# Head of a fused Mamba and mixture-of-experts kernel: early B and C loads, softplus ahead of the third gate, four C products by VectorE

## The chip, the cores and the metric

The kernel runs on one core of one Trainium2 chip. The metric is device time in microseconds (us) of one execution, the median over runs. Engine names are those of the profile: PE is TensorE (PEld its weight loads), DVE is VectorE, ACT is ScalarE, POOL is GpSimd, SP is SyncE, whose queue (SPq) issues most of the DMAs.

## The reference

Two branches read the same layer-normed input of 4096 tokens with 256 features, and their product is added to the input. All is float32.

```
xn = layernorm(x)                          # x: (2, 2048, 256)
u  = silu(conv4(in_proj_x(rmsnorm(xn))))   # 512 channels
dt = softplus(dt_proj(x_proj_dt(u)));  B, C = x_proj_BC(u)   # 16 states
h_t = exp(dt_t * A) * h_{t-1} + (dt_t * u_t) * B_t           # per channel and state
y_t = sum_s h_t[s] * C_t[s] + D * u_t
s  = xn + out_proj(y * silu(z));  s = s + mlp(rmsnorm(s))
g  = silu(top2_of_8_experts(xn))
out = x + s * g
```

## The kernel before

Tokens are cut into 8 blocks of 512 (c = 0 to 7, four to a sequence), channels into 4 groups of 128 (d), and the 16 states into 8 pairs (g). One scan step n is one (c, d, g): 256 steps. A step makes the input b = du*B on DVE (L1498), two hardware scans on DVE (L1502), one per state, needs two exponentials da from ACT (L1387), which run two steps ahead (LEAD), then the product with C (L1430, in `times_c`, on POOL, the last step on DVE), for most steps from n = 8 the sum of the pair on POOL (L1432), and PE adds the states into PSUM with the identity (L1400). `save` (L1424) keeps the last column of h for the next block.

All work of one engine stands in one order, the order in which the Python program emits it. Three things set that order. Before the scan loop a list of calls is written out by hand (from L1249): `norm`, `logits`, `layer_norm`, `gate` and `scatter_group` for the tokens, `go(k)`, which takes k pieces of the generator `front(0)`, and `tick()`, which lets deferred work (`later`) fall due. In the loop, after each of the 512 half steps, `draw` takes 1.93 us worth of PE work from the first of five lists that has any: `pre` (the last gate and the tables of the experts), `zs` (`gate_z`), `projs` (`out_proj`), `chain` (`front`), `side` (the 39 expert tiles and 16 tiles of the MLP; `side` waits until `pre` is empty). Deferred work falls due some half steps after it was put.

The parts that the change touches or that the prediction follows:

- `norm(b)` scales a block of x on ACT (L277) and transposes it on PE (L288) into PSUM: even blocks into the tile `b` that later holds the scan's input, odd blocks into `du` and `y`. `logits(b)` copies the transposes to SBUF on ACT (L295), stores them (L297) and computes the expert logits on PE (L300). `layer_norm(b)` writes the layer-normed block (blocks 2 to 7 on ACT, L315) and stores it (L321).
- `gate(g)` (L405 to L444) chooses two experts for 1024 tokens on DVE, with two matmuls for the counts (L421, L424); its first operation that reads the counts is a copy, L428. `scatter_group(g)` sends those tokens to their experts' rows by 16 indirect DMAs issued by POOL (L462).
- `front(c)`: four input projections on PE (L621), convolution taps (ACT L631 to L638, DVE L646), SiLU on ACT (L660), `project_x` (PE L666, ACT copy L671, store of B and C to DRAM `bcd`, L673), then per channel group the softplus: `exp_v` (PE L685, ACT L693 to L699, a subtraction L700) and `log_v` (ACT logarithm L707, then L712 and L713 make dt). For c = 0, d = 0 and 1, L700, L712 and L713 run on DVE, otherwise on POOL.
- `load_bc` (L762) loads two rows of `bcd`, broadcast to 128 partitions (512 KB), into the tiles B0 to B7 and C0 to C7. Blocks 0 to 5 of x lie in B0 to B5 at the start, and the transposed blocks 2 to 7 in C2 to C7; B6, B7, C0 and C1 are free.
- `gate_z` (PE L772, ACT L781, L787, L794, DVE L783) makes the gate silu(z).
- `routed` (list `pre`): the last `layer_norm`s and gate 3, the last scatters, `tiles_of_experts` and `rows_of_results` (DVE, L502 to L598), `fill_up` (zeros behind each expert's rows, L604, SPq), and the first expert's loads. An expert reads its rows (L1035), transposes them (PE L934, ACT copy L937) and runs two matmul layers (PE L946 and L958, ACT L1053).

Of the kernel before, what the change touches and what calls it, by code (L numbers as in the profile page):

```python
# [9 lines left out]
F32 = mybir.dt.float32  # L10
# [8 lines left out]
P = 128  # L19
T = 512  # L20
# [32 lines left out]
def kernel(  # L53
# [135 lines left out]
    def with_exp():  # L189
        if table[0] == WITH_SILU:  # L190
            act_table(WITH_TANH)
# [81 lines left out]
    def norm(b):  # L273
        xr = work.tile([P, J, DM], F32, tag="h", name=f"xr{b}")
        for j in range(J):
            i = b * J + j
            nc.scalar.activation(  # L277
                xr[:, j, :], x_of(b, j), AF.Identity,
                scale=both_norms[:, i : i + 1], bias=off[:, i : i + 1],
            )  # L280
        if b % 2:
            pt = [ps_1.tile([P, T], F32, tag=tag, name=f"pt{b}_{tag}") for tag in ("du", "y")]
        else:
            both = ps_b.tile([P, KM, T], F32, tag="b", name=f"pt{b}")
            pt = [both[:, k, :] for k in range(KM)]
        for k in range(KM):
            for j in range(J):
                nc.tensor.transpose(pt[k][:, ts(j, P)], xr[:, j, ts(k, P)], ident)  # L288
        pts[b] = pt

    def logits(b):
        pool, tag = (bcp, f"C{b}") if b > 1 else (rows, "xrT")
        xrT[b] = pool.tile([P, KM, T], F32, tag=tag, name=f"xrT{b}")
        for k in range(KM):
            nc.scalar.copy(xrT[b][:, k, :], pts[b][k])  # L295
        if b > 1:
            nc.sync.dma_start(xrd[b], xrT[b])  # L297
        for j in range(J):
            for k in range(KM):
                nc.tensor.matmul(  # L300
                    lgp[:, b * J + j, :], xrT[b][:, k, ts(j, P)], gw_sb[:, k, :],
                    start=(k == 0), stop=(k == KM - 1),
                )

    def layer_norm(b):

        for j in range(J):
            i = b * J + j
            if b < GB:
                nc.gpsimd.tensor_scalar(  # L310
                    x_of(b, j), x_of(b, j), rstd[:, i : i + 1], moff[:, i : i + 1],
                    ALU.mult, ALU.add,
                )
            else:
                nc.scalar.activation(  # L315
                    x_of(b, j), x_of(b, j), AF.Identity,
                    scale=rstd[:, i : i + 1], bias=moff[:, i : i + 1],
                )
        per = J // len(xts[b])
        for k, xn in enumerate(xts[b]):  # L320
            nc.sync.dma_start(xnd[b][:, ts(k, per), :], xn)  # L321
# [150 lines left out]
    def scatter_group(g):  # L472
        for i in range(g * GI, (g + 1) * GI):
            for k in range(TOPK):
                scatter(i, k)
# [138 lines left out]
    def front(c):  # L614
# [48 lines left out]
        def project_x():  # L663
            px, n = bank("h", [DR + 2 * DS, T], f"pxd{c}")
            for d in range(ND):
                nc.tensor.matmul(  # L666
                    px, xp_sb[:, d, :], xcs[c, d], start=(d == 0), stop=(d == ND - 1)
                )
            xd = rows.tile([DR + 2 * DS, T], F32, tag="xd", name=f"xd{c}", bufs=1)
            bcd[c] = dram.tile([2 * DS, T], F32, tag="bcd", name=f"bcd{c}")  # L670
            later.put(lambda: nc.scalar.copy(xd, px), n)  # L671
            later.put(
                lambda: nc.sync.dma_start(bcd[c], xd[DR : DR + 2 * DS, :]), ("bcd", c), after=3  # L673
            )
            return xd, n

# [79 lines left out]
    def load_bc(c, g, which_ones="BC"):  # L756
        later.free("bcd", c)
        for which in which_ones:
            i = "BC".index(which)
            t = bcp.tile([P, 2, T], F32, tag=f"{which}{g}", name=f"{which}{c}_{g}")  # L760
            r = i * DS + 2 * g
            nc.sync.dma_start(  # L762
                t, bcd[c][r : r + 2, :].unsqueeze(0).to_broadcast([P, 2, T])
            )
            bct[c, which, g] = t
# [475 lines left out]
            later.put(total, after=1 if self.c == NBLK - 1 else 2)  # L1241


    def tick():
        later.now += 1
        later.run()
# [20 lines left out]
    def go(pieces):  # L1267

        for _ in range(pieces):
            next(first)  # L1270
# [25 lines left out]
    logits(4)  # L1296
    tick()
    go(3)
    logits(5)
    layer_norm(4)  # L1300
    layer_norm(5)
    tick()
    norm(6)
    gate(2)
    scatter_group(2)
    tick()
    norm(7)
    go(4)
    logits(6)
    tick()  # L1310
    logits(7)
    assert 0 in bcd and (0, 1) in dt_made
    for which, gs in (
        ("B", (0, 1, 6, 7)), ("C", range(DS // 2)), ("B", (2, 3, 4, 5)),
    ):
        for g in gs:
            load_bc(0, g, which)

# [20 lines left out]
        for _ in ffns[0].rows():  # L1339
            pass  # L1340


    hs, ys, y_n, hts, das, dus = {}, {}, {}, {}, {}, {}

    def all_ffn(upto):

# [24 lines left out]
    zs, projs, chain = [], [], []  # L1371
    side = []
    pre = []

    NS = NBLK * ND * (DS // 2)
    at = [(c, d, g) for c in range(NBLK) for d in range(ND) for g in range(DS // 2)]

    def exps(n, q):
        if n >= NS:
            return  # L1380
        c, d, g = at[n]
        begun[0] = n
        assert (c, d) in dt_made
        if q == 0:
            das[n] = work.tile([P, 2, T], F32, tag="da", name=f"da{c}_{d}_{g}", bufs=3)
        with_exp()
        nc.scalar.activation(  # L1387
            das[n][:, q, :], dts[c, d], AF.Exp, scale=a_neg[:, d, 2 * g + q : 2 * g + q + 1]
        )

    def accumulate(n):
        c, d, g = at[n]
# [28 lines left out]
    def save(n):  # L1421
        c, d, g = at[n]
        if c % CPB != CPB - 1:
            nc.gpsimd.tensor_copy(hs[c][:, d, 2 * g : 2 * g + 2], hts[n][:, :, T - 1])  # L1424

    def times_c(n):
        c, d, g = at[n]

        engine = nc.vector if n == NS - 1 else nc.gpsimd
        engine.tensor_tensor(hts[n], hts[n], bct[c, "C", g], ALU.mult)  # L1430
        if paired(n):
            nc.gpsimd.tensor_tensor(hts[n][:, 0, :], hts[n][:, 0, :], hts[n][:, 1, :], ALU.add)  # L1432
# [24 lines left out]
                share -= got  # L1457
        return min(share, 0.0)

    LEAD = 2  # L1460
    LAG = 3
    BACK = 3
    HALF = 1.93

    pre.append(routed())
    side.append(all_ffn(None))
    for n in range(LEAD):
        for q in range(2):
            exps(n, q)
    owed = 0.0  # L1470
    for n in range(NS):
        c, d, g = at[n]
        if n == 3:
            chain.append(first)
        if d == 0 and g == 0 and c % CPB != CPB - 1:
            hs[c] = small.tile([P, ND, DS], F32, tag="hs", name=f"hs{c}")
        if d == 0 and g == (1 if c else 4):
            zs.extend(gate_z(c, k) for k in range(ND))
        if c + 1 < NBLK:
            if d == 0 and g == 1 and c:  # L1480
                xrT[c + 1] = rows.tile([P, KM, T], F32, tag="xrT", name=f"xrTr{c + 1}")
                nc.sync.dma_start(xrT[c + 1], xrd[c + 1])
            if d == 0 and g == 4:
                chain.append(front(c + 1))
        if c > 0 and d == 0 and g == 0:
            projs.append(out_proj(c - 1))
        if n == NS - 4:
            projs.append(out_proj(NBLK - 1))
        for q in range(2):
            later.now += 1  # L1490
            if q == 0:
                if g == 0:
                    assert (c, d) in dt_made
                    dus[c, d] = ps_1.tile([P, T], F32, tag="du", name=f"du{c}_{d}")
                    nc.vector.tensor_tensor(dus[c, d], dts[c, d], xcs[c, d], ALU.mult)
                hts[n] = work.tile([P, 2, T], F32, tag="h", name=f"h{c}_{d}_{g}")
                inp = ps_b.tile([P, 2, T], F32, tag="b", name=f"b{c}_{d}_{g}")
                nc.vector.tensor_tensor(  # L1498
                    inp, dus[c, d].unsqueeze(1).to_broadcast([P, 2, T]),
                    bct[c, "B", g], ALU.mult,  # L1500
                )
            nc.vector.tensor_tensor_scan(  # L1502
                hts[n][:, q, :], das[n][:, q, :], inp[:, q, :],
                0.0 if c % CPB == 0 else hs[c - 1][:, d, 2 * g + q : 2 * g + q + 1],
                ALU.mult, ALU.add,
            )
            if q == 0 and n > 0:
                save(n - 1)
                times_c(n - 1)
            exps(n + LEAD, q)  # L1510
            later.run()
            if q == 0 and n >= LAG:
                sums(n - LAG)
            if q == 0:

                past = n - BACK
                if past >= 0 and at[past][1] == ND - 1 and at[past][0] + 1 < NBLK:
                    load_bc(at[past][0] + 1, at[past][2])
            owed = draw(HALF + owed)
# [66 lines left out]
```

## Time and profile before

| what | value |
|---|---|
| median of 3 runs | 1506.11 us (1504.72 to 1514.64) |
| the profiled execution | 1505.4 us; its span 1503.7 us |
| PE busy | 1347.4 us (90% of the span), mean granted clock 0.944 |
| DVE busy | 1217.2 us (81%) |
| POOL busy | 1188.3 us (79%) |
| ACT busy | 978.5 us (65%), 121 table loads of 1283 ns |
| scan loop begins / PE full from / last y | about 100 us / 170 us / 1460 us |

A row of a timeline gives start, duration, engine, line, operation, output from inputs, shapes, count, and in brackets the idle time of the engine ahead of it with what ended it ("remote" is a signal whose sender the profile doesn't know). A row of the chain gives start, duration and what lay on the chain that ended last. A row of windows gives, for a stretch, each engine's busy time with its instruction count in brackets, then PE's granted clock, the DMA share and GB/s.

### The profile page before, as it was taken

The page shows a single profiled execution, that of the slowest core. Times are in us where ns is not written, and L with a number is a line of the kernel's source. Part 1 is how long each engine was busy: PE and PEld are TensorE (multiplying, and loading weights), DVE is VectorE, ACT ScalarE, POOL GpSimd, SP SyncE. Part 2 cuts the span into 40 slices and gives each one's busy share as a digit, 9 for nine tenths or more (in the row PEclk, how much of TensorE's full clock was granted, in tenths as well). Part 3 has the DMA queues.
Part 4 walks back from the last instruction along what each step waited for, and adds up shares of the span by engine and source line. Part 5 has one row for each costly group of instructions (what it writes and reads, how often), then busy time and mean ns, then how long its engine had stood idle before and what let it go on. Part 6 is the DMA issues. An engine that isn't in the chain of part 4 may idle for free.

```text
span 1503.7 us, 18025 instructions
## 1 busy us (share of the span) xinstructions
PE 1347.4 (90%) x5122; PEld 944.1 (63%) x5122; DVE 1217.2 (81%) x1351; ACT 978.5 (65%) x1765; POOL 1188.3 (79%) x964
## 2 busy tenths in 40 slices
PE   5744799999999999999999999979878998999958
PEld 4531467765776677766776677546655666667726
DVE  7448888889798998799888988999767967888853
ACT  4742777458655776568656865677648988778932
POOL 2665779987898799968997899889975888777860
PEclk9556899999999999999999999999999999999989
DMA  5568134962477345924492449445830116412110
GB/s 187 198 234 304 46 99 145 306 220 76 125 230 280 92 131 180 335 95 121 158 363 74 129 140 331 167 139 175 268 114 8 55 53 211 139 53 60 57 57 14
DMA packets 169317, 231.85 MB, mean 154 GB/s; under 512 B 19825, under 2 KB 139761, under 8 KB 169217
## 3 DMA queue, kind: packets, MB, share of 16 engines
q1 hardware_dynamic: 163072, 213.91, 42.9%
q0 software_dynamic: 6144, 16.79, 3.4%
q8 instruction: 41, 0.67, 0.2%
q14 instruction: 60, 0.48, 0.1%
HBM read 195.12 MB, written 35.52 MB: 153 GB/s over the span
## 4 chain that ended last, share of the span: by engine, by line
PE 44%; POOL 25%; DVE 10%; ACT 10%; issue 6%; DMA 4%; another core or an unknown queue 1%; POOLq 0%; DVEq 0%; SPq 0%; ACTq 0%
POOL h L1430 13%; PE phe L946 9%; PE y L1400 8%; PE poe L958 8%; POOL h L1432 6%; PE pom L958 4%; PE phm L946 4%; PE po L821 3%; ACT L183 2%; PE px L621 2%; DVE h L1502 2%; DMA B<-bcd 2%; ACT da L1387 2%; PE pz L772 2%; DMA C<-bcd 1%
## 5 line engine op out<-in xcount | busy, mean ns | idle before, releaser
L1430 POOL TENSOR_TENSOR h<-h,C 128x1024 f32<-128x1024 f32 x255 | 604.1, 2371 | 36.7 <-issue 11.5
L1502 DVE TENSOR_TENSOR_SCAN h<-da,hs,b 128x512 f32<-128x512 f32 x384 | 477.6, 1270 | 41.4 <-PE y L1400 10.8
L1387 ACT ACTIVATE da<-dt,a_neg 128x512 f32<-128x512 f32 x512 | 352.8, 717 | 93.3 <-DVE h L1502 87.2
L1400 PE MATMUL y<-h,ident 128*128 128x512 f32 x596 | 307.3, 617 | 34.6 <-POOL h L1432 17.5
L1498 DVE TENSOR_TENSOR b<-du,B 128x1024 f32<-128x1024 f32 x256 | 315.0, 1231 | 18.4 <-DMA B<-bcd 9.1
L1432 POOL TENSOR_TENSOR h<-h 128x512 f32<-128x512 f32 x214 | 275.4, 1287 | 16.8
L946 PE MATMUL phe<-xsTe,w_e 128*128 128x256 f32 (+1 forms) x1248 | 268.1, 366 | 9.4 <-ACT xsTe L937 7.6
L946 PEld LDWEIGHTS phe<-xsTe,w_e 128*128 128x128 f32 x1248 | 225.4, 194 | 72.7 <-issue 27.6
L958 PE MATMUL poe<-w_e,hide 128*128 128x256 f32 x1136 | 265.2, 380 | 2.5 <-ACT hide L1053 2.5
L958 PEld LDWEIGHTS poe<-w_e,hide 128*128 128x128 f32 x1136 | 213.8, 190 | 65.1 <-issue 33.5
L1053 ACT ACTIVATE hide<-phe,b 128x256 f32<-128x256 f32 (+1 forms) x312 | 123.6, 450 | 140.8 <-PE phe L946 140.4
L1400 PEld LDWEIGHTS y<-h,ident 128*128 128x128 f32 x596 | 112.2, 197 | 124.0 <-issue 60.5
L1502 DVE TENSOR_TENSOR_SCAN h<-da,b 128x512 f32<-128x512 f32 x128 | 151.3, 1210 | 12.7 <-PE y L1400 4.8
L183 ACT ACT_TABLE_LOAD x121 | 155.2, 1283 | 2.9 <-PEq L1573 0.8
L946 PE MATMUL phm<-xsTm,w_m 128*128 128x256 f32 x512 | 121.0, 387 | 2.7 <-ACT hidm L1144 2.0
L1424 POOL COPY hs<-h 128x2 f32<-128x2 f32 x192 | 42.0, 219 | 100.9 <-DVE h L1502 89.4
L958 PE MATMUL pom<-w_m,hidm 128*128 128x256 f32 x512 | 121.0, 386 | 0.0
L946 PEld LDWEIGHTS phm<-xsTm,w_m 128*128 128x128 f32 x512 | 99.1, 194 | 29.6 <-issue 10.8
L958 PEld LDWEIGHTS pom<-w_m,hidm 128*128 128x128 f32 x512 | 98.5, 194 | 25.2 <-issue 12.5
L462 POOL DMA_INDIRECT xs_d<-xt,slot x64 | 64.0, 1000 | 49.1 <-issue 21.4
L646 DVE SCALAR_TENSOR_TENSOR xc<-px,par_sb,xc 128x512 f32<-128x512 f32 x96 | 71.6, 748 | 30.4 <-ACT xc L638 25.6
L1185 POOL DMA_INDIRECT yk<-ys_d,row_y x60 | 58.3, 972 | 22.6 <-issue 14.2
(221 smaller groups left out, 1366.7 us busy)
## 6 DMA issues: line engine op xcount, KB each, us to landing
w_e<-in_w SPq DMA_DIRECT2D x312, 256.0 KB
B<-bcd SPq DMA_DIRECT2D x64, 512.0 KB
C<-bcd SPq DMA_DIRECT2D x64, 512.0 KB
xs<-xs_d SPq DMA_DIRECT2D x32, 256.0 KB
ys_d<-ys SPq DMA_DIRECT2D x32, 256.0 KB
b<-in_b SPq DMA_DIRECT2D x39, 128.0 KB
xnr<-xnd SPq DMA_DIRECT2D x16, 256.0 KB
xom<-in_x SPq DMA_DIRECT2D x16, 256.0 KB
```

What stands on the lines that cost most here:

```text
L183: nc.scalar.preload_act_table_set(name)
L462: r = nc.gpsimd.indirect_dma_start(out=xs_d, out_offset=bass.IndirectOffsetOnAxis(ap=slot[:, k, i : i + 1], axis=0), in_=x_of(i // J, i % ...
L646: nc.vector.scalar_tensor_tensor(v[:, s : s + T], px, conv_w[:, d, KC - 1 - s : KC - s], v[:, s : s + T], ALU.mult, ALU.add,)
L946: nc.tensor.matmul(ph[:, q, :], self.w1[c0 // 2][:, k, ts(q, P)], self.xT[:, k, :], start=(k == 0), stop=(k == KM - 1),)
L958: nc.tensor.matmul(po[:, j, :], self.hid[c // 2][:, c % 2, ts(j, P)], self.w2[c // 2][:, c % 2, :], start=(c == 0 and j == 0), stop=(c == ...
L1053: nc.scalar.activation(hc[:, q, :], ph[:, q, :], AF.Relu, bias=self.b1[:, c0 + q : c0 + q + 1])
L1387: nc.scalar.activation(das[n][:, q, :], dts[c, d], AF.Exp, scale=a_neg[:, d, 2 * g + q : 2 * g + q + 1])
L1400: nc.tensor.matmul(ys[c, d], ident, hts[n][:, q, :], start=False, stop=(g == DS // 2 - 1 and q == nq - 1),)
L1430: engine.tensor_tensor(hts[n], hts[n], bct[c, "C", g], ALU.mult)
L1432: nc.gpsimd.tensor_tensor(hts[n][:, 0, :], hts[n][:, 0, :], hts[n][:, 1, :], ALU.add)
L1498: nc.vector.tensor_tensor(inp, dus[c, d].unsqueeze(1).to_broadcast([P, 2, T]), bct[c, "B", g], ALU.mult,)
L1502: nc.vector.tensor_tensor_scan(hts[n][:, q, :], das[n][:, q, :], inp[:, q, :], 0.0 if c % CPB == 0 else hs[c - 1][:, d, 2 * g + q : 2 * g ...
```

## The change

- For block 0 the store of B and C to `bcd` is put one tick behind `project_x`'s copy instead of three, and B0, B1, B6, B7, C0 and C1 are loaded right there, ahead of `logits(5)`; the other ten loads stay behind `logits(7)`, C2 to C7 first.
- A tick, `go(4)` and a tick (softplus of d = 0 and 1) come ahead of `layer_norm(4)`, and the first four exponentials behind `layer_norm(5)`; `gate(2)` and `scatter_group(2)` follow, and then `norm(6)` and `norm(7)`. Before, `norm(6)` stood ahead of gate 2, and the softplus' end and the exponentials behind it.
- The product with C of steps 0 to 3 moves from POOL to DVE, and the saved column of those steps from POOL to ACT.
- `first` (the rest of block 0's `front`, d = 2 and 3) joins its list at step 2 instead of 3, `gate_z` of block 0 at g = 1 instead of 4, `front(1)` at g = 2 instead of 4.

`hs`, `ys` and their like, LEAD, NS, `at` and `exps` are only moved up in the file. ScalarE's SiLU is used in both kernels.

```
             later.put(
-                lambda: nc.sync.dma_start(bcd[c], xd[DR : DR + 2 * DS, :]), ("bcd", c), after=3
+                lambda: nc.sync.dma_start(bcd[c], xd[DR : DR + 2 * DS, :]),
+                ("bcd", c), after=3 if c else 1,
             )
...
     go(3)
+    for which, gs in (("B", (0, 1, 6, 7)), ("C", (0, 1))):
+        for g in gs:
+            load_bc(0, g, which)
     logits(5)
+    tick()
+    go(4)
+    tick()
+    assert (0, 1) in dt_made
     layer_norm(4)
     layer_norm(5)
-    tick()
-    norm(6)
+    for n in range(LEAD):
+        for q in range(2):
+            exps(n, q)
     gate(2)
     scatter_group(2)
+    norm(6)
+    norm(7)
     tick()
-    norm(7)
-    go(4)
     logits(6)
     tick()
     logits(7)
-    assert 0 in bcd and (0, 1) in dt_made
-    for which, gs in (
-        ("B", (0, 1, 6, 7)), ("C", range(DS // 2)), ("B", (2, 3, 4, 5)),
-    ):
+    for which, gs in (("C", range(2, DS // 2)), ("B", (2, 3, 4, 5))):
...
         if c % CPB != CPB - 1:
-            nc.gpsimd.tensor_copy(hs[c][:, d, 2 * g : 2 * g + 2], hts[n][:, :, T - 1])
+            engine = nc.scalar.copy if n < 4 else nc.gpsimd.tensor_copy
+            engine(hs[c][:, d, 2 * g : 2 * g + 2], hts[n][:, :, T - 1])
...
-        engine = nc.vector if n == NS - 1 else nc.gpsimd
+        engine = nc.vector if n in (0, 1, 2, 3, NS - 1) else nc.gpsimd
         engine.tensor_tensor(hts[n], hts[n], bct[c, "C", g], ALU.mult)
...
-    for n in range(LEAD):
-        for q in range(2):
-            exps(n, q)
...
-        if n == 3:
+        if n == 2:
             chain.append(first)
...
-        if d == 0 and g == (1 if c else 4):
+        if d == 0 and g == 1:
             zs.extend(gate_z(c, k) for k in range(ND))
...
-            if d == 0 and g == 4:
+            if d == 0 and g == (4 if c else 2):
                 chain.append(front(c + 1))
```

More of the change, by code (lines that the diff above doesn't have):

```diff
@@ L1241, in finish, with exps @@
             later.put(total, after=1 if self.c == NBLK - 1 else 2)
+    hs, ys, y_n, hts, das, dus = {}, {}, {}, {}, {}, {}
+    LEAD = 2
+    NS = NBLK * ND * (DS // 2)
+    at = [(c, d, g) for c in range(NBLK) for d in range(ND) for g in range(DS // 2)]
+    def exps(n, q):
+        if n >= NS:
+            return
+        c, d, g = at[n]
+        begun[0] = n
+        assert (c, d) in dt_made
+        if q == 0:
+            das[n] = work.tile([P, 2, T], F32, tag="da", name=f"da{c}_{d}_{g}", bufs=3)
+        with_exp()
+        nc.scalar.activation(
+            das[n][:, q, :], dts[c, d], AF.Exp, scale=a_neg[:, d, 2 * g + q : 2 * g + q + 1]
+        )
     def tick():
@@ L1340, in routed @@
             pass
-    hs, ys, y_n, hts, das, dus = {}, {}, {}, {}, {}, {}
     def all_ffn(upto):
@@ L1373 @@
     pre = []
[L1375 to L1389, printed above, removed]
     def accumulate(n):
@@ L1458, in draw @@
         return min(share, 0.0)
-    LEAD = 2
     LAG = 3
```

## The prediction

> **What bounds the kernel now.** I read the page's slices first, then windows by stage, then the chain and the timelines of the first 200 us, where the change lies. The windows show a head that nothing fills and a body that PE fills: from 200 to 1430 us PE is busy for 1170.71 of 1230 us, from 100 to 170 us for 32 of 70.
>
> ```profile
> 100.00:125.00 25.00, 10.61 (x14) 3.77 (x14) 16.83 (x40) 3.48 (x6) 19.23 (x19) 0.50 1.03 412
> 125.00:146.00 21.00, 11.63 (x20) 4.80 (x20) 19.68 (x58) 7.40 (x14) 12.21 (x11) 0.71 0.78 265
> 146.00:170.00 24.00, 9.79 (x21) 5.15 (x22) 21.45 (x24) 16.48 (x26) 17.52 (x15) 0.67 0.22 72
> 170.00:200.00 30.00, 30.00 (x110) 20.86 (x110) 25.41 (x26) 15.18 (x34) 19.75 (x16) 0.98 0.29 84
> 200.00:1430.00 1230.00, 1170.71 (x4539) 827.00 (x4538) 1049.93 (x966) 856.56 (x1529) 1046.13 (x816) 0.98 0.48 155
> ```
>
> So the question is how much sooner PE fills up. The timeline of DVE carries the head; each row below ends a wait, or is slow for its size.
>
> ```profile
> 86.16 0.23 DVE L428 COPY halves<-bank_lg 128x64 f32<-128x64 f32 x1 [9.02 <-remote]
> ...
> 90.33 0.69 DVE L712 TENSOR_TENSOR ls<-ex,ls 128x512 f32<-128x512 f32 x1
> ...
> 100.47 1.23 DVE L1498 TENSOR_TENSOR b<-du,B 128x1024 f32<-128x1024 f32 x1 [6.78 <-DMA B<-bcd]
> 101.81 1.22 DVE L1502 TENSOR_TENSOR_SCAN h<-da,b 128x512 f32<-128x512 f32 x1
> 102.95 0.20 DVE L405 TENSOR_TENSOR halves<-bank_lg,unr 128x64 f32<-128x64 f32 x1
> ...
> 120.90 1.23 DVE L1498 TENSOR_TENSOR b<-du,B 128x1024 f32<-128x1024 f32 x1 [2.35 <-DMA B<-bcd]
> ...
> 129.18 2.36 DVE L535 TENSOR_SCALAR scratch<-steps,scratch 128x39 f32<-128x39 f32 x1
> ...
> 136.91 2.27 DVE L567 SCALAR_TENSOR_TENSOR scratch<-scratch,ends 128x8 f32<-128x8 f32 x1
> ```
>
> Gate 3 (102.95) stands behind the first scan, which waited for B0, though its logits were done at 98.49 (PE L300 begins at 91.43 and takes 7.06). On ACT and PE two more waits hang on the same order: the softplus' logarithm behind gate 2, and PE behind the late gate z.
>
> ```profile
> 89.67 1.23 ACT L707 ACTIVATE ex<-ex 128x512 f32<-128x512 f32 x2 [9.24 <-DVE ls L700]
> ```
>
> ```profile
> 157.39 3.78 PE L621 MATMUL px<-xrT,in_sb 128*128 128x512 f32 x4 [14.20 <-DVE sz L783]
> ```
>
> **The change, part by part.** I move rows of this profile to the changed order. T is the end of the expert tables on DVE (L598), 145.6 us now.
>
> *Softplus ahead of gate 2.* ACT is done with L699 at 75.1 as now; its table load (1.28) and two L707 (1.23) end at 77.6 instead of 90.9. DVE's six softplus operations (L700, L712, L713, 4.1 us) end at 79.9, so gate 2 begins at 79.9 instead of 73.44, 6.5 us later. That costs nothing because L428 sat 9.02 us idle: 16 operations of about 0.26 us bring DVE to it at 84.1. PE's two count matmuls (1.2 us at half clock) allow 85.2, the old row says 86.16. Gate 2 therefore ends at 87 to 88.9 (now 88.95), and the scatters of group 2 start with it. If that cover were gone, the price would be the 6.5 us.
>
> *ACT's order up to logits 7.* From 77.6: eight L315 (4.0), four exponentials (2.6, dt is there at 79.9), eight L277 (4.1), to 88.3; the transposes (PE, 2 us a block at half clock, behind the count matmuls) follow it; four L295 to 90.4 or so; the 32 logit matmuls (7.06) end at 96.4 instead of 98.49. The layer norms of blocks 4 and 5 come at 77.6 to 81.6 instead of 62 to 66, ahead of the scatter that needs them at 87.
>
> *Loads.* The store of `bcd` follows ACT's copy (L671, 60.56), now past one store of transposes on SPq instead of two and two layer-norm stores. Six loads of 512 KB need the scatters of group 0 (last issued at 57.22) and take 7.7 us at the 408 GB/s of the stretch 100 to 110. With the worst wait from issue to use in the head (11.62 us, the chain's row at 109.19) they are there by 76, where b needs them at 91. The stores that they push back (L297 of block 5, L321 of blocks 4 and 5) are needed first by C5, B4 and B5, after 95. So the wait of 6.78 goes. What is late next is the PSUM tile du, which block 7's transposes hold until ACT's copy (90 to 91): du, b0 and the first scan end at about 93.6, still ahead of the logits. Gate 3 then begins at 96.4 instead of 102.95: 6.5 us sooner. B2 is issued behind C7 (which needs logits 7), at about 100 instead of 109.19; two stores and seven loads, 4.5 MB, at 300 to 412 GB/s, put it at 103 to 107. b2 needs it at 112, so the 2.35 goes too.
>
> *Four C products on DVE, z sooner.* From the second scan of step 0 to L502 takes 12.9 us now (111.57 to 124.49), 4.5 of it waits. It gains two C products and L783 (0.67). For a C product the rows give 1.23 (L1498, as large) and twice L712 less overlap, 1.3, beside scatters; at the far end 2.46 (DVE's one C product, at 1445.42, while POOL ran another). I take 1.3, because POOL then only issues scatters, as beside L712. The stretch becomes 12.2 us, 14.3 if the odd 2.11 us ahead of step 1 stays; I take 13.2, so 0.3 us lost.
>
> *Expert tables.* L535 and L567 took 2.36 and 2.27 where their like take 0.2. POOL's C products ran at exactly these times:
>
> ```profile
> 129.16 2.35 POOL L1430 TENSOR_TENSOR h<-h,C 128x1024 f32<-128x1024 f32 x1
> ...
> 136.82 2.34 POOL L1430 TENSOR_TENSOR h<-h,C 128x1024 f32<-128x1024 f32 x1
> ```
>
> Those two products are now DVE's, so 21.1 us become 16.9: 4.2 us gained. Zero if POOL's next operation falls there. T moves from 145.6 to 135.2 (6.5 - 0.3 + 4.2 = 10.4 us).
>
> *PE's start.* Now PE waits at 157.39 because three z banks were taken and freed by L783 behind the tables. In the new order all z and both dt matmuls lie ahead of T, and px0 waits only for step 2's C product on DVE (b, scan, product, 3.9 us behind T) and its two sums (3.8 at half clock): px0 at T + 7.7 instead of T + 11.8. From px0 to y1 (L1396, 197.67) PE needs 40.3 us; one z (1.9) leaves that stretch and eight expert matmul records (1.7) enter it. So y1 comes at T + 47.8 instead of T + 52.1: 4.3 us more. The first expert's rows don't hold it: the scatters end about 130 instead of 136.5 without POOL's three products between them.
>
> *Small things.* Four saved columns on ACT (0.2 each) wait for scans whose da buffers ACT's next exponential waits for anyway. Four more table loads (125 instead of 121), 5.1 us on an engine 65% busy; the bounds are 0 and 5.1, I take 0.
>
> **The sum.** y1 comes 10.4 + 4.3 = 14.7 us sooner; if PE then stays the bound, the 1.7 us of expert work done ahead also counts (16.4); if the scan on DVE is, its shift at step 10 is 10.4 + 2.5 = 12.9. Middle: 14.7. Against the profiled execution's 1505.4 that is 1490.7, say 1491; its median stands at 1506.11, 0.7 higher.
>
> **A rule against it.** DVE's product of 1445.42 took twice its size's time beside POOL's. The Trainium skill, page "SBUF — State Buffer", section "Who interferes with whom", explains such a row: a VectorE instruction with two SBUF inputs and a GpSimd instruction that reads SBUF lock each other out of a shared read interface, and the second blocks fully. By that, the two products behind T could meet POOL's softplus subtractions, and the sum would be 2.4 us less, 1493.
>
> **The rivals.**
> - *Late signals again.* Twice PE's transposes were reported late: DVE sat until 60.62 and 86.16 although the count matmuls ended by 54.4 and 79.3, both beside a run of scatters. The new gate 2 has its counts ahead of the transposes, but norm 6 follows at once. If its signal comes 6.4 us late again (84.7 for 78.3), copies shift from 88.4 to about 94.5, gate 3 to 102.2, and the gain shrinks by 5.8: 1497. Against it: POOL has no scatter to issue from 83.8 to 87.
> - *Slower: held as long as the scatters run.* Both waits ended 2.4 us behind POOL's last scatter (58.20 and 83.77). The new transposes of block 7 end at 88.4, inside the next run (87 to 108 at 1.285 each). Held until 110, block 7's copies and logits would end at 115.5 and gate 3 would start 19 us later than in my sum: 1510. It decides as soon as the hold lasts 15 us. Against it: logits and dt matmuls at 61 to 73 were on time beside scatters.
> - *DVE becomes the bound.* All four products at 2.46: 4.8 us, 1496.
> - *Given back later.* The drawn order is redealt throughout (expert tiles start up to four scan steps sooner). Between blocks the chain leaves PE for ACT and DVE (337 to 363 us now: taps, table loads, SiLU), so a new order can lose or gain some 10 us: 1481 or 1501.
>
> **How the numbers follow.** My sum (1488 to 1494) 0.4, better by a luckier order (1481 to 1488) 0.12, late signals or slow products (1494 to 1499) 0.22, given back (1499 to 1506) 0.14, held signals or a worse order (over 1506) 0.12. One per cent, about what a measurement can tell from no change, lies at 1491 and 1521. Faster by over 1%: half of the first case, the second, and a little: 0.37. Slower by over 1%: 0.07. The range for 8 in 10 leaves out 0.08 at the bottom and 0.11 on top: 1482 to 1507; my sum's own range is 1488 to 1494.
>
> **What would show it.** L707 at 76 to 78 us with no wait; b0 without a wait for B; L405 of gate 3 at 96 to 97 (102 with late signals, 115 if held); L535 and L567 near 0.2 us; DVE's C products at 1.2 to 1.3 us; px0 without a wait for L783; the first expert transposes near 147 instead of 164; L1396 of y1 near 183 instead of 197.67, and about the same lead at 400 and 1400 us. The forecast is wrong if gate 3 starts after 102, or if that lead melts by 1000 us.

## The result and the profile after

The changed kernel takes 1514.9 us (1514.12 to 1516.57) where the kernel before takes 1506.16 on the same chip: a ratio of 1.0059, 95% interval 1.0041 to 1.0077. The forecast of 1491 is 24 us too low, and the time lies above its range. The profiled execution has a span of 1512.4 us (1503.7 before).

The same stretches as before the change show where the lead was lost:

```profile
100.00:125.00 25.00, 9.69 (x18) 4.06 (x18) 14.93 (x31) 5.33 (x9) 19.20 (x20) 0.64 0.79 309
125.00:146.00 21.00, 8.96 (x16) 3.29 (x16) 13.02 (x51) 12.53 (x21) 5.65 (x6) 0.74 0.43 152
146.00:170.00 24.00, 12.63 (x29) 6.93 (x30) 22.82 (x28) 9.98 (x20) 11.39 (x9) 0.72 0.43 130
170.00:200.00 30.00, 30.00 (x118) 21.70 (x118) 28.40 (x29) 16.73 (x37) 22.48 (x19) 1.00 0.37 110
```

From 125 to 146 us DVE, the engine that should be writing the tables without a break, is busy for 13.02 of 21 us (19.68 before). Up to there the timeline of DVE is as forecast: no wait of 9 us at gate 2, gate 3 at 97.33, a product with C in 1.20 us.

```profile
85.95 0.22 DVE L428 COPY halves<-bank_lg 128x64 f32<-128x64 f32 x1 [1.12 <-issue]
...
97.33 0.23 DVE L405 TENSOR_TENSOR halves<-bank_lg,unr 128x64 f32<-128x64 f32 x1 [4.66 <-PE bank_lg L300]
...
111.20 1.20 DVE L1440 TENSOR_TENSOR h<-h,C 128x1024 f32<-128x1024 f32 x1
```

Then the tables of the experts begin, 4.8 us sooner than before (119.65 for 124.49), and stop:

```profile
119.65 0.14 DVE L502 CAST end_of<-ends 128x8 int32<-128x8 f32 x1
...
124.07 0.17 DVE L505 TENSOR_SCALAR scratch<-scratch 128x8 f32<-128x8 f32 x1 [4.21 <-remote]
125.46 0.43 DVE L508 TENSOR_TENSOR over<-scratch,steps 128x256 f32<-128x256 f32 x1 [1.22 <-issue]
...
129.66 0.17 DVE L516 SCALAR_TENSOR_TENSOR scratch<-scratch 128x8 f32<-128x8 f32 x1 [2.19 <-remote]
...
148.67 0.23 DVE L598 TENSOR_TENSOR row_y<-scratch 128x64 uint32<-128x64 f32 x1
```

They take 29.2 us instead of the 16.9 of the sum. In the kernel before they took 21.2 and began without a wait (rows of its timeline, then the end as a row of its chain):

```profile
124.49 0.31 DVE L502 CAST end_of<-ends 128x8 int32<-128x8 f32 x1
...
124.85 0.17 DVE L505 TENSOR_SCALAR scratch<-scratch 128x8 f32<-128x8 f32 x1
125.06 0.50 DVE L508 TENSOR_TENSOR over<-scratch,steps 128x256 f32<-128x256 f32 x1
```

```profile
145.48 0.23 DVE row_y L598
```

In the changed kernel the profile puts DVE's waits down to its own results, to signals without a sender, or to nothing ("issue"). ACT and PE stand still beside it, ACT from 121.8 to 131.8 us, PE from 123.3 to 132.4, just behind this copy of ACT:

```profile
131.76 0.58 ACT L788 COPY sz<-pz 128x512 f32<-128x512 f32 x1 [9.98 <-remote]
132.40 3.42 PE L773 MATMUL pz<-xrT,in_sb 128*128 128x512 f32 x4 [9.12 <-issue]
```

The end of the tables, T, is 148.9 us (145.7 before). The scan regains its old times by step 10 (187.01 for 187.21), though PE has then done 12 expert products and 4 transposes more. So no lead is left at 200 us. A second loss comes late: until 1140 us the scan is level within 6 us, and by step 236 it is 12.8 us behind.

Two things in the runs need a word. They fell on six chips. On three (the first among them) the kernel before takes 1504.9 to 1506.2 us, on the other three 1489.9 to 1492.2; the 14 us lie ahead of block 1. The run e3 below, with the head of the kernel before, begins block 1 at 278.4 us on a faster chip, where the kernel before itself has no trace, against 292.4. From block 1 on, the twelve runs with the old order there take 1207.9 to 1213.2 us, on either kind. Of the run with the old order from step 32 only the part from block 1 on is read from the profile, since that execution began gate 2 at 96.5 us instead of 81 and took 1521.5 where its others took 1498.8 to 1507.3.

### The profile page after: what moved, and what is told of

Same layout as the page of the kernel before. It is cut to its first block, busy times and chain, and to the rows that moved or that the text cites. A ratio compares the mean times of both kernels' runs of the same rounds, so it can differ in the third digit from the quotient of the medians.

```text
span 1512.4 us, 18013 instructions
## 1 busy us (share of the span) xinstructions
PE 1351.6 (89%) x5122; PEld 946.1 (63%) x5122; DVE 1218.7 (81%) x1355; ACT 983.9 (65%) x1773; POOL 1176.1 (78%) x956
## 4 chain that ended last, share of the span: by engine, by line
PE 50%; POOL 19%; DVE 13%; ACT 11%; issue 5%; another core or an unknown queue 1%; DMA 0%; POOLq 0%; DVEq 0%
PE phe L947 10%; PE poe L959 10%; PE y L1409 10%; POOL h L1440 9%; POOL h L1442 4%; PE po L822 4%; DVE h L1508 4%; PE phm L947 3%; ACT L183 3%; PE pom L959 3%; PE pz L773 2%; DVE b L1504 2%; ACT da L1261 2%; PE px L621 2%; DVE xc L646 2%
## 5 line engine op out<-in xcount | busy, mean ns | idle before, releaser
L1440 POOL TENSOR_TENSOR h<-h,C 128x1024 f32<-128x1024 f32 x251 | 592.9, 2363 | 35.3 <-issue 9.1
L1442 POOL TENSOR_TENSOR h<-h 128x512 f32<-128x512 f32 x214 | 275.7, 1288 | 16.8
L1054 ACT ACTIVATE hide<-phe,b 128x256 f32<-128x256 f32 (+1 forms) x312 | 123.0, 449 | 135.2 <-PE phe L947 134.2
L1508 DVE TENSOR_TENSOR_SCAN h<-da,b 128x512 f32<-128x512 f32 x128 | 151.4, 1211 | 10.2 <-PE y L1409 2.6
```

The costliest lines, as they stand in the source:

```text
L1054: nc.scalar.activation(hc[:, q, :], ph[:, q, :], AF.Relu, bias=self.b1[:, c0 + q : c0 + q + 1])
L1508: nc.vector.tensor_tensor_scan(hts[n][:, q, :], das[n][:, q, :], inp[:, q, :], 0.0 if c % CPB == 0 else hs[c - 1][:, d, 2 * g + q : 2 * g ...
```

## The experiments

Theories, named in the expectations. For the standstill in the tables: A, GpSimd issuing scatters with no other work between them holds the other engines' signals; B, it comes from DMA traffic or fetched code, whoever does the products; F, it depends on the chip or the execution. For the late loss: C, the count by which the experts' and the MLP's work stands ahead of the scan; D, something else that the changed head leaves; E, their exact order from block 1 on; G, that order in blocks 6 and 7 alone; H, in all blocks evenly.

All runs in one table. "Tables" is L502 to L598 on DVE, "rest" the span from the first scan of block 1 (step 32) to the end; both in us, from the profiled executions.

| run | ratio to before, 95% interval | tables | block 1 begins | rest |
|---|---|---|---|---|
| *chips with standstills* | | | | |
| kernel before | 1 | 124.5–145.7 | 292.4 | 1211.3 |
| changed kernel | 1.0059, 1.0041–1.0077 | 119.7–148.9 | 289.1 | 1223.3 |
| e5 changed, again | 1.0093, 1.0076–1.0110 | 126.0–151.2 | 291.8 | 1223.8 |
| e6 old order from 32 | 0.9988, 0.9974–1.0001 | | | 1211.3 |
| e7 same, products on POOL | 0.9938, 0.9921–0.9955 | 122.3–146.5 | 286.6 | 1207.9 |
| e8 early loads, softplus only | 0.9986, 0.9977–0.9996 | 121.6–142.9 | 289.7 | 1211.4 |
| e9 old order from 188 | 1.0006, 0.9994–1.0018 | 120.7–148.8 | 290.4 | 1214.4 |
| e10 before, ahead from 187 | 1.0064, 1.0044–1.0085 | 125.7–146.5 | 293.7 | 1219.5 |
| e11 before, products on DVE | 1.0038, 1.0021–1.0055 | 126.7–148.8 | 298.1 | 1209.6 |
| e12 changed, spaced scatters | 0.9991, 0.9977–1.0005 | 120.2–137.2 | 279.4 | 1223.4 |
| *chips without* | | | | |
| e1 changed, products on POOL | 0.9991, 0.9973–1.0008 | 104.4–125.7 | 265.6 | 1221.0 |
| e2 changed, two draws less | 1.0043, 1.0023–1.0063 | 106.6–126.1 | 267.7 | 1231.8 |
| e3 before, two draws more | 1.0082, 1.0065–1.0098 | 110.8–131.4 | 278.4 | 1219.6 |
| e4 changed, old places | 0.9975, 0.9961–0.9989 | 106.4–126.0 | 275.3 | 1209.4 |
| e13 spaced, old order from 32 | 0.9951, 0.9934–0.9967 | 106.8–123.9 | 271.5 | 1213.2 |
| e14 before, groups 0, 1 spaced | 1.0043, 1.0026–1.0060 | 109.9–128.5 | 287.5 | 1209.1 |
| e15 all spaced, old order | 1.0071, 1.0054–1.0088 | 105.5–122.5 | 288.8 | 1210.2 |
| e16 as e13, half the pause | 0.9925, 0.9909–0.9942 | 105.1–122.3 | 265.7 | 1211.0 |
| e17 as e13, again | 0.9950, 0.9933–0.9966 | 106.2–122.8 | 273.5 | 1210.8 |
| e18 as e14, again | 1.0052, 1.0036–1.0069 | 108.3–125.3 | 286.6 | 1211.6 |

**e1, the products back on GpSimd.**

```
-        engine = nc.vector if n in (0, 1, 2, 3, NS - 1) else nc.gpsimd
+        engine = nc.vector if n == NS - 1 else nc.gpsimd
```

with the saved columns on GpSimd likewise.

> The changed kernel with the first four products with C and the first four saved columns back on GpSimd; all else as changed. In the changed kernel GpSimd issued 32 scatters with nothing between them (23 from 88.8 to 117.4 us, 9 from 119.2 to 129.6), and VectorE, ScalarE and TensorE stood still for 12 us of 119.7 to 133.9; in the kernel before the same stretch ran through, and there GpSimd had products among its scatters. Theory A, unbroken scatter issuing holds the other engines' signals: here the tables of the experts (count row to fill-up row) take 17 to 22 us instead of 29, and their end comes at 136 to 142 instead of 148.8; the time falls by the part of that lead that lives on, 0 to 8 us, to 1507 to 1515. Theory B, the stall belongs to the DMA traffic or to the code that is fetched there, whoever does the products: the tables take 27 to 31 us, and the time is 1513 to 1519.

Tables of 21.3 us look like theory A, but on this chip e2, with the products on DVE, took 19.5 and had no wait in them (one row, L597, took 2.70 us beside a subtraction of POOL, L701; the rest took 16.8). The run settles nothing about the standstill; it shows that without one the place of the products is worth little: block 1 begins at 265.6 and 267.7.

**e2 and e3, moving the side work against the scan.** e2, in the changed kernel, and e3, in the kernel before:

```
+            if n == 40:
+                continue
             owed = draw(HALF + owed)
```

```
-            owed = draw(HALF + owed)
+            owed = draw(HALF * (2 if n == 40 else 1) + owed)
```

> The changed kernel, in which scan step 40 deals out no side work. In the changed kernel the work of the experts and of the MLP stands 8 matrix products further ahead of the scan from the second channel half on; after this edit it stands level with the kernel before (0, in four places 2 to 4 behind). Theory C, the 9 us that are lost between scan steps 206 and 255 come from that place of the MLP's work against the scan (a gate that waits for rows gathered behind a late start on GpSimd): they go, and the time is 1502 to 1508. Theory D, they come from something else that the changed head left behind: the time stays within 1512 to 1517.

> The kernel before, in which scan step 40 deals out two shares of side work more, so that the work of the experts and of the MLP stands mostly 8 matrix products further ahead of the scan, as in the changed kernel; its head is that of the kernel before. Theory C (the place of the MLP's work against the scan costs the 9 us at the end): 1510 to 1517. Theory D (the place is indifferent): 1501 to 1507.

e3 confirms that two draws more cost the kernel before 12 us (1504.47 against 1492.21). Its trace, of an execution of 1499.62 us, shows 8.3 of them, most in block 4 (161.2 for 153.4) and none in block 6 (192.9 for 193.6). e2 fails theory C: level in count, it lost even more, 20.5 us of rest over the kernel before, most in blocks 3 (165.3 for 157.4) and 5 (171.9 for 165.4) and none in block 6 (193.5). A level count is not the old order: which share is dealt at which step still differed.

**e4, the old places.**

```
-        if n == 2:
+        if n == 3:
             chain.append(first)
-        if d == 0 and g == 1:
+        if d == 0 and g == (1 if c else 4):
             zs.extend(gate_z(c, k) for k in range(ND))
-            if d == 0 and g == (4 if c else 2):
+            if d == 0 and g == 4:
                 chain.append(front(c + 1))
```

> The changed kernel with the first projection, the gate columns z of block 0 and the front of block 1 begun at their old scan steps (3, 4, 4 instead of 2, 1, 2); early loads of B and C, early softplus and the four products on VectorE stay. From the second channel half on the order of the side work is then exactly that of the kernel before. Theory C: the late loss goes, and of the changed head stays what its tables of the experts leave: end of tables 140 to 149, time 1500 to 1507. Theory D: 1511 to 1517. For the stall in the tables: if it is the unbroken scatter issuing (theory A) they still take 25 to 30 us here; if it comes from the gate columns and the front that now run at the same time, 17 to 22.

With the exact old order the late loss is gone: rest 1209.4, and the kernel is faster than before by 0.25%. The tables (19.5 us) say nothing on this chip.

**e5 to e8, on one chip with standstills.** e5 is the changed kernel itself, e7 is e6 with e1's edit, e8 is e4 with e1's edit. e6:

```
-            owed = draw(HALF + owed)
+            owed = -0.28 if n == 32 else draw(HALF + owed)
```

> The changed kernel as it is, on the chip on which the two kernels with its head that came before had no standstill in the tables of the experts (their end at 125.5 and 126.1 us). Theory A (unbroken scatter issuing always holds the signals): the tables take 25 to 30 us here too, ratio 1.005 to 1.008 to the kernel before. Theory F (the standstill is met by chance of a chip or an execution, the order of the side work is what always costs): tables of 17 to 20 us, end at 124 to 128, blocks 1 to 7 and the tail together about 1223 us against 1211 in the kernel before, ratio 0.998 to 1.003.

> The changed kernel, in which scan step 32 deals out nothing and the account of the side work is then set to what the kernel before has there; from there on every engine's instructions stand in exactly the order of the kernel before. Block 0 keeps the changed order, with the early columns z and the early front. Theory E, the order of the side work against the scan from block 1 on is what costs: blocks 1 to 7 and the tail take 1207 to 1213 us (as in the kernel before, and with the gate columns and fronts at their old places: 1209.5), and the time is 1480 to 1487, ratio 0.991 to 0.997. Theory D, something else that the changed head leaves behind costs it: they take 1218 to 1232, ratio 0.999 to 1.004.

> As the run with the old order from step 32 on, and the first four products with C and the saved columns on GpSimd again. Theory E: blocks 1 to 7 and the tail 1207 to 1213 us. The products on VectorE are worth little either way: with GpSimd's products block 1 began 2 us sooner (265.7 against 267.7 us) in two kernels that differ in them, so 1478 to 1486. If VectorE's products are a gain, this is 2 us or more above the run with them.

> The kernel before with the early loads of B and C and the early softplus alone: gate columns, first projection and front at their old scan steps, the four products and saved columns on GpSimd. From the second channel half on the order is that of the kernel before. If the early loads and softplus carry the gain, 1485 to 1490, as the run with the products on VectorE (1487.9); if VectorE's products carry it, 1490 to 1494.

e5 fell on another chip than e1 to e4, not on theirs as its expectation has it. It stood still again (tables 25.2 us, the first gap 4.2 as in the first trace) and its rest is the same to 0.5 us. So the standstill belongs to chip and kernel (F for which chip, A or B for what), and the late loss to the order whatever the chip. e6 shows E: nothing but the dealing at step 32 was changed, and the rest falls from 1223.8 to 1211.3, that of the kernel before. The medians agree (1504.54 for 1519.11), and so do e7, e13, e16 and e17 with the same edit (rest 1207.9 to 1213.2). The ratio of e6 missed the expected 0.991 to 0.997, for no lead was left of the head: e5, which has the same one, begins block 1 only 0.6 us ahead of the kernel before. e7, which differs from e6 in the products and saved columns alone, has a median 8.1 us lower; it begins block 1 5.2 us sooner than e5. With POOL's products among the scatters no wait over 0.9 us is left in the tables. They still take 24.2 us, because other rows now grow:

```profile
136.10 2.38 DVE L558 TENSOR_TENSOR scratch<-scratch 128x39 f32<-128x39 f32 x1
```

beside this product on POOL:

```profile
136.07 2.35 POOL L1439 TENSOR_TENSOR h<-h,C 128x1024 f32<-128x1024 f32 x1
```

L558's other row takes 0.20 in the same profile. That agrees with the Trainium skill, page "SBUF — State Buffer", section "Who interferes with whom": a VectorE instruction with two SBUF inputs and a GpSimd one that reads SBUF lock each other out. e8 is faster by 0.14%; the early loads and softplus alone are worth about 2 us there.

**e9 and e10, where the order costs.** e9 in the changed kernel, e10 in the kernel before:

```
-            owed = draw(HALF + owed)
+            owed = -1.19 if (n, q) in ((187, 1), (188, 0)) else draw(HALF + owed)
```

```
             owed = draw(HALF + owed)
+            if n == 187:
+                draw(2 * MM)
```

> The changed kernel, in which the two shares by which its side work stands ahead are taken back only at scan step 188, ahead of block 6, so that from there on the order is that of the kernel before; blocks 1 to 5 keep the changed order. Blocks 1 to 7 and the tail took 1211.3 us in the kernel before, 1223.2 and 1223.8 in the changed one, 1211.2 with the old order from step 32. Theory G, the 12 us are lost in blocks 6 and 7, where the MLP's gates and table loads stand against the scan (block 6: 203.0 against 193.6 us): here 1210 to 1215. Theory H, they are spread over all blocks: 1216 to 1221.

> The kernel before, with four pieces of side work more dealt out at scan step 187, so that in blocks 6 and 7 the side work stands 8 matrix products ahead, as in the changed kernel; head and blocks 0 to 5 as before. Theory G: block 6 takes 199 to 204 us, blocks 1 to 7 and the tail 1219 to 1225, ratio 1.005 to 1.009. Theory H: 1211 to 1215, ratio 1.000 to 1.003.

For the changed kernel's order it is theory G: taking the lead back only ahead of block 6 leaves 3.1 of the 12.0 us (1214.4), and giving it there alone costs 8.2 (1219.5). Its block 6 alone is 9.4 us longer than in the kernel before; its blocks 1 to 5 differ by up to 5.2 us either way and sum to 1.8. Other shifts lose elsewhere, as e2 and e3 did. Block 6 in the windows of the kernel before, the changed one, e9 and e10, in this order:

```profile
1084.84:1278.42 193.58, 172.73 (x612) 116.57 (x611) 149.38 (x143) 153.24 (x241) 151.51 (x132) 0.95 0.29 95
```

```profile
1083.37:1286.40 203.03, 180.24 (x625) 119.43 (x624) 151.19 (x143) 162.28 (x253) 152.39 (x131) 0.94 0.28 93
```

```profile
1086.71:1277.35 190.64, 170.47 (x612) 114.95 (x611) 149.38 (x144) 152.16 (x241) 149.07 (x130) 0.96 0.28 96
```

```profile
1088.10:1290.21 202.11, 177.50 (x612) 117.13 (x612) 151.15 (x143) 161.45 (x252) 150.99 (x130) 0.94 0.27 93
```

The same 612 matmuls fill 172.73 or 177.50 us, and ACT has 11 instructions more in 202.11 us than in 193.58: 41 table loads for 38 (42 in the changed kernel), 1.28 us each. What a load more may mean can be seen in the changed kernel's waits of DVE from 1150 to 1370 us; the first row of POOL is the start of the knot, the last of DVE its end:

```profile
1196.75 0.20 POOL L230 TENSOR_TENSOR rms<-rms 128x4 f32<-128x4 f32 x1 [5.84 <-ACT rms L892]
```

```profile
1216.00 0.63 ACT L1208 ACTIVATE yk<-yk 128x512 f32<-128x512 f32 x1 [8.33 <-POOL yk L1204]
```

```profile
1216.66 0.69 DVE L1229 SCALAR_TENSOR_TENSOR pom<-yk,pom 128x512 f32<-128x512 f32 x1 [8.67 <-ACT yk L1208]
```

POOL waits 5.84 us for a norm that ACT does late, behind SiLU pairs and their loads; behind it stand four gathers, four softplus operations and two products with C; then POOL's sum of the gathered rows, ACT's tanh, and with it the scan's engine. Such waits of DVE for gathered rows sum to 16.6 us in this stretch, 8.3 in the kernel before:

```profile
DVE pom L1229 <- ACT yk L1208: 16.6, 3, 8.7
```

```profile
DVE pom L1228 <- ACT yk L1207: 8.3, 3, 4.2
```

No run takes the loads alone away, so this chain is read from the trace and not shown by an edit; that the order costs the time is.

**e11 and e12, the standstill.** e11 is the kernel before with the products on VectorE and the saved columns on ScalarE, that part of the change alone. e12, in the changed kernel:

```
         for i in range(NI - GI, NI):
             for k in range(TOPK):
                 scatter(i, k)
+            for _ in range(10):
+                nc.gpsimd.memset(spacer, 0.0)
```

where `spacer` is a tile of 16 columns that nothing reads.

> The kernel before with the first four products with C on VectorE and their saved columns on ScalarE, nothing else. The scatters of the last group then stand on GpSimd with no product between them. Theory A (unbroken scatter issuing holds the other engines' signals, on the chips that show such standstills: gate 2 there begins at 73 and ends at 86 us): the tables of the experts take 25 to 31 us instead of 20 to 21, block 1 begins 3 to 8 us later, ratio 1.002 to 1.006. On a chip without them, or by theory B (it does not matter who does the products): tables of 17 to 21 us, ratio 0.998 to 1.001.

> The changed kernel, with ten small fills of a tile that nobody reads on GpSimd behind every second scatter of the last group: some 1 us of pause each, no product, no other change. Theory A: on a chip with standstills the tables shrink from 25 to 29 us to 17 to 22 and their end comes 3 to 10 us sooner than in the changed kernel; ratio lower by 0.002 to 0.006 than the changed kernel's 1.006 to 1.009. Theory B (the standstill follows the DMA traffic, not the pace of the issuing): tables as in the changed kernel, 25 to 30 us. On a chip without standstills neither shows: tables of 17 to 20 us.

e12 came out as A forecast and not as B. POOL, in the changed kernel and in e12:

```profile
123.02 0.98 POOL L462 DMA_INDIRECT xs_d<-xt,slot  x1 [0.30 <-issue]
124.30 0.98 POOL L462 DMA_INDIRECT xs_d<-xt,slot  x1 [0.30 <-issue]
125.59 1.15 POOL L462 DMA_INDIRECT xs_d<-xt,slot  x1 [0.30 <-issue]
```

```profile
119.91 0.98 POOL L462 DMA_INDIRECT xs_d<-xt,slot  x1 [0.30 <-issue]
120.88 1.66 POOL L1358 MEMSET spacer<- 128x16 f32 x10
123.23 0.98 POOL L462 DMA_INDIRECT xs_d<-xt,slot  x1 [0.70 <-ACT scratch L449]
```

and DVE in e12, the same rows as in the changed kernel above:

```profile
120.19 0.19 DVE L502 CAST end_of<-ends 128x8 int32<-128x8 f32 x1
...
120.44 0.45 DVE L505 TENSOR_SCALAR scratch<-scratch 128x8 f32<-128x8 f32 x1
120.92 0.43 DVE L508 TENSOR_TENSOR over<-scratch,steps 128x256 f32<-128x256 f32 x1
...
136.99 0.23 DVE L598 TENSOR_TENSOR row_y<-scratch 128x64 uint32<-128x64 f32 x1
```

With a pause of 2.3 us behind every second scatter the tables run through in 17.0 us; block 1 begins at 279.4 us, 13.0 ahead of the kernel before. On the same chip e9, with the same head and no pauses, took 28.1 us for the tables and began block 1 at 290.4. So on such a chip the unbroken row of scatters is what brings the standstill on. The pauses spread the scatters' own transfers too, though, so whether the issuing or these transfers hold the other engines is not separated. e11 only half confirms theory A: the kernel is slower by 0.4% and block 1 begins 5.7 us later, but the tables took 22.1 us, 5 more than in e12 and not 25 to 31; the rest was lost behind them.

**e13 to e18, both losses taken away.** e13 and e17 are e12 with e6's edit; e16 has five fills instead of ten; e14 and e18 are the kernel before, and e15 is e13, with five fills behind every second scatter of groups 0 and 1:

```
             for k in range(TOPK):
                 scatter(i, k)
+            for _ in range(5 if g < 2 else 0):
+                nc.gpsimd.memset(spacer, 0.0)
```

> The changed kernel without both of the losses found: pauses behind the scatters of the last group, as in the run with spaced scatters, and the order of the side work of the kernel before from scan step 32 on. If the two are the whole of what went wrong: tables of the experts 16 to 18 us, block 1 begins at 279 to 283 us on a chip with standstills (279.4 with the pauses alone, against 291.8 in the changed kernel and 292.4 in the kernel before), blocks 1 to 7 and the tail 1208 to 1213, ratio 0.989 to 0.994, so about 1490 where the kernel before takes 1505. If a third loss is left: ratio 0.996 or more.

> The kernel before with five of the small fills behind every second scatter of groups 0 and 1, nothing else. There the second step of gate 1 waited 9.2 us to 60.6 and that of gate 2 9.0 us to 86.2, for signals that came late while 16 scatters were issued without a break. Theory A, the same cause as in the tables: these waits fall to under 4 us each and the second steps come at 52 to 57 and 74 to 81; the scatters of group 1 end some 8 to 12 us later, which takes back part: ratio 0.994 to 1.001. Theory B, these standstills come from elsewhere (code that is fetched, DMA traffic): the waits stay at 8 to 10 us, ratio 0.999 to 1.004.

> The changed kernel with the old order from scan step 32 on, ten small fills behind every second scatter of the last group, and five behind every second one of groups 0 and 1. If the standstills at gates 1 and 2 have the same cause, gate 3 begins 5 to 12 us sooner than with the last group's pauses alone (97.3 us), but the scatters end later (144 us there, 148 to 156 here) and the first expert's rows can not be read before: block 1 begins at 276 to 284 us, ratio 0.987 to 0.995. If the scatters' end decides, it is 2 to 8 us above the run with the last group's pauses alone.

> As the run with spaced scatters and the old order, with five small fills instead of ten behind every second scatter of the last group. With ten, the scatters ended at 137.5 us, 14 after the tables (123.9), and the first expert's rows can not be read before. If half the pause is still enough on a chip with standstills: tables 16 to 19 us, scatters done 6 to 9 us sooner, block 1 at 274 to 281 us, ratio 0.986 to 0.993. If the pause is too short: tables 22 to 28 us, ratio 0.993 to 0.999. On a chip without standstills: block 1 at 266 to 270, ratio 0.991 to 0.995.

> The run with spaced scatters (ten fills) and the old order once more, since the first was on a chip that shows no standstills (there block 1 began at 271.5 us, 3.8 us ahead of the one with the old places and without pauses, and the ratio was 0.995). On a chip with standstills, if the two losses are the whole: block 1 at 279 to 283, blocks 1 to 7 and the tail 1208 to 1213, ratio 0.989 to 0.994.

> The kernel before with spaced scatters in groups 0 and 1 once more, for a chip with standstills. Theory A: the second steps of gates 1 and 2 come at 52 to 57 and 72 to 81 us instead of 60.6 and 86.2, their waits fall under 4 us; the scatters end some 10 us later than the 136.5 of the kernel before, ratio 0.996 to 1.003. Theory B: the waits stay at 8 to 10 us, ratio 1.004 to 1.009. On a chip without standstills only the late end of the scatters shows, ratio 1.003 to 1.006.

All six runs fell on chips without standstills, so what e13 would give on one with them was not seen; e12's head and e6's rest, both measured, would sum to 279.4 + 1211.3 = 1490.7, an estimate. On these chips ten fills are too many: the scatters end at 137.5 and 138.2 us, 14 to 15 behind the tables, and the first expert's transposes begin 4.4 us behind the last scatter. With five they end at 130.4, block 1 begins at 265.7, and e16 is the fastest of all, 0.75% below the kernel before. The pauses have little part in that: e1 and e2 begin block 1 at 265.6 and 267.7 without any. On a chip with standstills the best run is e7, 0.62% below. e14, e15 and e18 have the late end of their scatters (145 to 155 us) and are slower by 0.4 to 0.7%; whether the waits at gates 1 and 2 have the cause of A stays open. DVE's waits there, in the kernel before and in e3, which has the same head on a chip without standstills:

```profile
DVE halves L428 <- remote: 18.2, 2, 9.2
```

```profile
DVE halves L428 <- PE bank_lg L424: 7.6, 2, 4.0
```

On that chip 32 scatters ran from 38 to 79 us in one piece in e1 and e2. Unbroken issuing alone is thus not enough; what else the first kind of chip has is not settled.

The traces of the two kinds also differ in what they hold. On the ten of the first kind no DMA issue has a landing time, and they record 16510 to 16927 semaphore events; the ten of the other kind have landing times and 18598 to 18774 events. Of what is missing, over half are landings of GpSimd's scatters and gathers. So a wait put down to "remote" or "issue" on the first kind may be one whose signal was not recorded; its length stands, its sender is open. Whether the recording has itself a part in the standstill no run shows.

## Why the prediction was wrong

- *Softplus ahead of gate 2, loads:* right. The logarithm begins at 76.53 without a wait (76 to 78 forecast), the 9.02 at gate 2 is 1.12, b0 waits for no load, gate 3 begins at 97.33 (96.4), 5.6 us sooner instead of 6.5.
- *Products on VectorE:* price right, 1.20 us each for 1.3. From gate 3 to L502 0.8 us were lost for 0.3.
- *Expert tables, "so 21.1 us become 16.9":* the step that failed. It counted the removal of POOL's products as gain alone. L535 and L567 fell to 0.24 and 0.17 as forecast, and with spaced scatters the tables take 17.0. But the same removal left the 32 scatters from 88.8 to 130.6 us with nothing between them, and DVE stood still for 12 us: the tables took 29.2, and T came at 148.9 instead of 135.2 (137.2 in e12). The rival "held as long as the scatters run" named such a hold and looked for it one stretch too early, at block 7's transposes. What in the scatters holds the other engines stays open.
- *PE's start:* direction right. px0 runs without its wait of 14.20, 7.0 us behind T (7.7 forecast). y1 comes at T + 49.0, and in e12 at T + 50.9, not T + 47.8: 1.2 to 3.1 us gained for 4.3.
- *The order:* counted at nothing in the sum, the second step that failed. It was the rival "given back later", whose size was right (some 10 us, measured 12.0). The blocks did shift throughout, by up to 5.2 us in blocks 1 to 5, but these nearly cancel; the net loss lies in block 6 (9.4 us).

The sum: of the 24 us, 9.7 are the standstill (289.1 against e12's 279.4; 11.0 against e9 on e12's own chip), 12.0 the order (1223.3 against 1211.3), 1.7 the head's lead itself (13.0 for 14.7).

## What to carry to other kernels

Where work is dealt out step by step, an early edit moves every later instruction against its neighbours; price that as its own term, by how much the tail moves when nothing but the dealing is shifted (here 8 to 20 us of 1211), and after an improvement ahead try to restore the old order behind it. Taking work off an engine that issues transfers also makes its transfers denser: ask what they then hold up. When a time differs between chips, find the stretch that differs before reading a wait there as something an edit can remove.

## What the runs showed of the hardware

- The same program differs by 14 us from chip to chip (1504.9 to 1506.2 or 1489.9 to 1492.2), all of it ahead of 293 us. On the slower kind DVE waits up to 9.2 us at gates 1 and 2, and beside the tables ACT and PE wait up to 10.0; on the faster kind the waits at the gates last up to 4.0 us.
- The traces from the slower kind miss about a tenth of the semaphore events (16694 in the changed kernel's, 18598 in e2's).
- On the slower kind ten small fills on GpSimd (1.66 us) behind every second scatter ended the standstill of the other engines, while the scatters kept their 0.98 us each.
- Behind the head the chips agree to 0.4%: the old order gives a rest of 1207.9 to 1211.4 us in five traces from the slower kind and 1209.1 to 1213.2 in seven from the faster.
